# An attention-and-MLP kernel: one item's denominators by another road, one eviction issued earlier, one projection a piece later

## The chip, the cores and the metric

The kernel runs on one core of a Trainium2 chip. A core has a matrix engine (TensorE, "PE" in the profile, with its weight loads as "PEld"), VectorE ("DVE"), ScalarE ("ACT"), GpSimd ("POOL") and SyncE ("SP"), which here only issues DMAs. Each engine works through its own queue in order, and they tell each other of finished work by semaphores. Matrix products write to PSUM, which has eight banks of 512 fp32 numbers per partition; everything else lives in SBUF or in DRAM. The metric is the device time of one execution in microseconds, as the median of the runs.

## The reference, cut to what matters

The input `x` has 16 elements of 256 channels by 32 x 32 positions, so each element is a matrix of 256 channels by S = 1024 positions. All is fp32. Two layers follow one another:

- Layer 0 is an attention with 4 heads of 64 channels: q, k and v by one matrix with a bias, softmax of q times k over the keys, times v, an output matrix `w_out`, and the input added.
- Layer 1 starts with a group norm over 32 groups, then an attention with 8 heads of 32 channels, an output matrix, and its input added; then a second group norm and an MLP of 256 to 1024 to 256 channels with an exact GELU, and its input added.

```python
attn = jax.nn.softmax(jnp.einsum('bihd,bjhd->bijh', q, k) * SCALE, axis=2)
res = jnp.einsum('bijh,bjhd->bihd', attn, v).reshape(B, S, N_HEADS * D_K)
res = res @ w_out + b_out + xs
```

The softmax is computed as exponentials, their sums (the denominators), and a multiplication of the result by the denominators' reciprocals. The kernel takes no maximum off; it keeps running totals of the denominators and of their reciprocals, and runs a general version afterwards if one of them has left the safe range.

## The kernel before, in words

`first_pass` handles the elements b = 0 to 15 one after another. The stages of one element overlap those of its neighbours, and the order is written out by hand: a stage is a Python generator or a list of small functions ("pieces"), and `run` and `run_pieces` call one piece after another. After each piece, `later.tick()` counts down what was put off with `later.after(n, fn)`: fn runs n pieces later. The program text that results is then given to a planner, which lays the instructions into each engine's queue by its own estimate of when each is ready; what stands earlier in the text goes first among those ready. `tc.keep_in_program_order` and `tc.issue_after` tie an instruction behind others of its engine. The waits between engines follow from the tiles that the instructions write and read. The queues in the trace are therefore not exactly the order of the text.

**The first attention** (`attention_a`) has four items per element: two blocks t of 512 positions times two channel halves c. Items are numbered i = 0 to 3 as (t, c) = (0,0), (0,1), (1,0), (1,1). Each item runs over 8 blocks of keys. For each, `scores` forms s_a (line 434) and its exponential e_a (line 444, ScalarE), and two steps later `weigh` accumulates acc_a (line 457, TensorE) and sums the exponentials into es_a (line 471, VectorE). After the last block the result is copied and added from PSUM (lines 477 and 478).

**Its denominators** go one of two roads. The usual one, `denominators` (lines 375 to 406), copies den from PSUM (line 376), spreads four rows of it over 128 partitions by a DMA (line 381), takes the reciprocal of the small 128 x 16 tile (line 387), writes it to DRAM as rows (line 398) and reads these rows back, broadcast to partitions (line 403); two small additions on GpSimd keep the totals (lines 399 and 400). Its `waits` are two numbers of pieces: from the spread to the reciprocal, and from there to the multiplication. `normalise` takes this road for both items of a block t at once, and `scale` multiplies (line 541). The other road, `normalise_item` (lines 489 to 508), is for element 0's block t = 1 alone. It treats each item by itself: den's products (line 493), the reciprocal of the whole 128 x 512 tile on VectorE (line 504), the multiplication (line 505), and `add_to_range` three pieces later, two reductions on VectorE (line 417) and two additions on GpSimd (line 418). For item 2 den is first copied to SBUF (line 502).

**The projections** are made by `out_proj`: o after the first attention, j after the second. Its function `issue` multiplies by the output matrix (`part`, instructions at line 357 through `product`) and evicts with `leave`. A projection of one block t has two column blocks co, each the sum of two products kc. There are two forms. With `apart`, each co has a bank of its own tile, and the order is co by co, each evicted directly. Otherwise both co lie in the two banks of one tile, a "wide" tile; there are three wide tiles, used in turn, and the scores s_b of the second attention use them too. `leave` is on ScalarE (line 781, into a spare tile) where a spare tile is there, which is the case for j of block 0 in elements 1 to 14, and else on VectorE (line 787), with the statistics of the group norm behind it (line 790).

**Between the two attentions** of an element stand, for elements 1 to 14, the previous element's first MLP stage (`hidden`, 12 pieces: begin, middle and finish for each of four parts in pairs; rows "m" of line 1146) and the making of q and k with seven products instead of eight (`qk_by_seven`, line 1052). The second projection of the first attention, o for t = 1, is put off into these pieces by `later.after` in `scale` (line 543). Its statistics start the group norm that makes the second attention's input gn_g.

**The second attention** (`attention_b`) forms s_b (line 602), e_b (line 615), sums es_b (line 630) and acc_b (line 656). Between its units, filler pieces run: the second MLP stage of the previous element, and v of the next one.

Of the kernel before, what the change touches and what calls it, by code (L numbers as in the profile page):

```python
# [259 lines left out]
def first_pass(ctx, tc, x, out, k):  # L260
    nc = tc.nc
    B, C, S = x.shape
    CC, SB, NT = C // P, S // P, S // TB
    HC = k["m1b"].shape[1]
    later = Later()
# [44 lines left out]
    def wide(name, n=None):  # L310
        if n is None:
            n = next(m for m in order if m not in kept)
        use(n)
        return ps_s.tile([P, 2, TB], F32, tag=f"s{n}", name=name)

    def bank(name, n):
        return ps_a.tile([P, TB], F32, tag=f"b{n}", name=name)
# [36 lines left out]
    def product(o, w, r, **flags):  # L354
        for c0 in range(0, P, cols[0]):
            sl = slice(c0, c0 + cols[0])
            nc.tensor.matmul(o[sl], w[:, sl], r, **flags)  # L357
# [17 lines left out]
    def denominators(key, den, d, full, waits, then, parts=1):  # L375
        nc.scalar.copy(d, den)
        n = full.shape[1]
        w = 4 * TB // P
        spread = work.tile([P, w], F32, tag="spread", name=f"sp_{key}", bufs=2)
        row = dram.tile([4 * TB // n, n], F32, tag="row", name=f"row_{key}", bufs=4)  # L380
        nc.sync.dma_start(
            spread, d[:: 32 // parts].rearrange("p (a b) -> p a b", b=w)
        )

        def invert():
            inverse = work.tile([P, w], F32, tag="inverse", name=f"inv_{key}", bufs=2)
            tc.keep_in_program_order(nc.vector.reciprocal(inverse, spread))
            if parts > 1:
                num = P // parts
                for r in range(parts):  # L390
                    nc.sync.dma_start(
                        row[:, r * n // parts : (r + 1) * n // parts].rearrange(
                            "g (a b) -> g a b", b=w
                        ),
                        inverse[r * num : (r + 1) * num],
                    )
            else:
                nc.sync.dma_start(row.rearrange("r (a b) -> (r a) b", b=w), inverse)
            nc.gpsimd.tensor_add(dsum, dsum, spread)
            nc.gpsimd.tensor_add(isum, isum, inverse)  # L400
            num = P * n // (4 * TB)
            for r in range(P // num):
                spread_out["last"] = nc.sync.dma_start(
                    full[r * num : (r + 1) * num], row[r].partition_broadcast(num)
                )
            later.after(waits[1], lambda: then(full))

        later.after(waits[0], invert)
# [5 lines left out]
    def add_to_range(den, inverse):  # L414
        for tot, what in ((dsum, den), (isum, inverse)):
            part = small.tile([P, 1], F32, tag="part", name="part")
            nc.vector.tensor_reduce(part, what, AX.X, ALU.add)
            nc.gpsimd.tensor_add(tot[:, :1], tot[:, :1], part)

    def attention_a(b, qT, kT, v, project):  # L420
        key, D, lag = f"a_{b}", D0, 2
        items = [(t, c) for t in range(NT) for c in range(CC)]
        units = [(i, kb) for i in range(len(items)) for kb in range(SB)]
        res = act.tile([P, CC, S], F32, tag="res", name=f"res_{key}")
# [64 lines left out]
        def normalise_item(i):  # L489
            t, c = items[i]  # L490
            den = wide(f"den_{key}_{i}", next(m for m in order if m != 2))[:, 0, :]
            for j in range(4):
                nc.tensor.matmul(
                    den[j * 32 : (j + 1) * 32, :], k["ones"], sums[i][:, j // 2, :],
                    start=True, stop=True,
                )
            if not c:
                homes.append(act.tile([P, CC, S], F32, tag="k1", name=f"d_{key}_{t}"))
            full, held_den = homes[0][:, c, :TB], homes[0][:, c, TB:]
            r = res[:, c, t * TB : (t + 1) * TB]  # L500
            if c < CC - 1:
                nc.scalar.copy(held_den, den)
                den = held_den
            tc.keep_in_program_order(nc.vector.reciprocal(full, den))
            tc.keep_in_program_order(nc.vector.tensor_mul(r, r, full))
            if c == CC - 1:
                later.after(2, lambda: project(t, res)())
            later.after(3, lambda: add_to_range(den, full))

        def normalise(t):  # L510
            half = TB // 2
# [23 lines left out]
        def scale(t, full):  # L535
            r = res[:, :, t * TB : (t + 1) * TB]
            halves = [
                y.rearrange(form, c=CC, h=2)
                for y, form in ((r, "p c (h q) -> p c h q"), (full, "p (h c q) -> p c h q"))
            ]  # L540
            tc.keep_in_program_order(nc.vector.tensor_mul(halves[0], *halves))
            if t == NT - 1:
                later.after(3 if b else 4, lambda: project(t, res)())

        cols[0] = 32
        pending = []
# [220 lines left out]
    def out_proj(key, w, src, bias, xs, t, stats, then):  # L767
        todo = list(range(CC))

        def issue(cos=range(CC), apart=False):  # L770
            home = None if apart else spare.pop("home", None)
            apart = apart or cols[0] == P
            if not apart:
                both = wide(f"{key}_{t}")
            ps = {}

            def leave(co):
                y = xs[:, co, t * TB : (t + 1) * TB]
                if home is not None:
                    held = home[:, 2 + co]  # L780
                    nc.scalar.activation(
                        held, ps[co], AF.Identity, bias=bias[:, co : co + 1]
                    )
                    later.after(1, lambda: add_up(co, y, held))
                    return
                else:
                    nc.vector.scalar_tensor_tensor(
                        y, ps[co], bias[:, co : co + 1], y, ALU.add, ALU.add
                    )
                nc.vector.bn_stats(stats[:, co, t, :], y)  # L790
                todo.remove(co)

            def add_up(co, y, held):
                with tc.issue_after(spread_out["es"].ins):
                    nc.vector.tensor_add(y, y, held)
                    nc.vector.bn_stats(stats[:, co, t, :], y)

            def part(co, kc):
                product(
                    ps[co],  # L800
                    w[:, kc, co * P : (co + 1) * P],
                    src(kc),
                    start=(kc == 0),
                    stop=(kc == CC - 1),
                )

            for co in cos:
                ps[co] = bank(f"{key}_{t}_{co}", co) if apart else both[:, co, :]
            if apart:
                for co in cos:  # L810
                    for kc in range(CC):
                        part(co, kc)
                    leave(co)
            else:
                for kc in range(CC):
                    for co in cos:
                        part(co, kc)
                for co in cos:
                    leave(co)
            if not todo and then:  # L820
                then()

        return issue
# [208 lines left out]
    def input_sums(key, y):  # L1032
        sums = weights_tile(f"qk7t_{key}")
        b11, b12 = (y[:, 0, t * TB : (t + 1) * TB] for t in range(NT))
        b21, b22 = (y[:, 1, t * TB : (t + 1) * TB] for t in range(NT))
        t1, t2, t3, t4 = (sums[:, n] for n in range(4))
        nc.vector.tensor_sub(t3, b22, b12)
        nc.vector.tensor_sub(t1, b12, b11)
        nc.vector.tensor_sub(t2, b22, t1)
        nc.vector.tensor_sub(t4, b21, t2)  # L1040
        return dict(t1=t1, t2=t2, t3=t3, t4=t4, b11=b11, b21=b21, b22=b22)
# [340 lines left out]
    for b in range(B):  # L1382
        def load_next(b=b):
# [3 lines left out]
            with tc.issue_after(spread_out["last"].ins):  # L1387
                load_blocks(1, b - 1)
                if b + 1 < B:
# [9 lines left out]
                lambda st, b=b, xn=xn, seven=seven, sums_1=sums_1: group_norm(  # L1399
                    f"g{b}", xs[b], st, k["g1w"], k["g1b"], "res", xn, 2 if b else 1,  # L1400
                    (lambda y: sums_1.update(input_sums(f"b{b}", y))) if seven else None,
                ),
# [62 lines left out]
        if first:  # L1465
# [10 lines left out]
                lambda st, b=b, hn=hn: group_norm(  # L1476
                    f"h{b}", xs[b], st, k["g2w"], k["g2b"], "q1", hn,
                    *((3 if b + 1 < B else 1), lambda y, b=b: sums_of_input(b, y)),
                ),
# [305 lines left out]
```

## Time and profile before

| | us |
|---|---|
| median of 3 runs | 3604.61 (3604.31 to 3605.24) |
| the profiled execution | 3603.56 |
| its span, first to last instruction | 3601.8 |
| TensorE busy | 3584.2 |
| VectorE busy | 2786.2 |
| ScalarE busy | 2283.0 |
| GpSimd busy | 219.1 |
| granted TensorE clock | 1.000 |

A row of the timeline gives start and length in us, the engine, the line of the kernel, the operation, output<-inputs by the program's names, and how many instructions were merged. In brackets stands how long the engine was idle before it, and what ended that. Names end in _a for the first attention and _b for the second; o and j are the projections, m the MLP. A product of fp32 numbers shows as two instructions, one for each pass. The ends of products are modelled, since products are pipelined: two rows of one engine may overlap by some 0.1 us, so starts are the better measure. From element 2 on, each element comes 222.4 to 223.8 us behind the one before it.

### The profile page before, as it was taken

The page shows a single profiled execution, that of the slowest core. Times are in us where ns is not written, and L with a number is a line of the kernel's source. Part 1 is how long each engine was busy: PE and PEld are TensorE (multiplying, and loading weights), DVE is VectorE, ACT ScalarE, POOL GpSimd, SP SyncE. Part 2 cuts the span into 40 slices and gives each one's busy share as a digit, 9 for nine tenths or more (in the row PEclk, how much of TensorE's full clock was granted, in tenths as well). Part 3 has the DMA queues.
Part 4 walks back from the last instruction along what each step waited for, and adds up shares of the span by engine and source line. Part 5 has one row for each costly group of instructions (what it writes and reads, how often), then busy time and mean ns, then how long its engine had stood idle before and what let it go on. Part 6 is the DMA issues. An engine that isn't in the chain of part 4 may idle for free.

```text
span 3601.8 us, 81991 instructions
## 1 busy us (share of the span) xinstructions
PE 3584.2 (100%) x35705; PEld 1470.2 (41%) x35705; DVE 2786.2 (77%) x3187; ACT 2283.0 (63%) x3196; POOL 219.1 (6%) x319
## 2 busy tenths in 40 slices
PE   9999999999999999999999999999999999999999
PEld 3334344343444434444344443434434444343433
DVE  5786877868788687876868878688786977868777
ACT  4665757667475675856658566585665757657572
POOL 4000100001000010000000000000000000000000
PEclk9999999999999999999999999999999999999999
DMA  3011311213122131221312213121121212213100
GB/s 130 8 57 33 78 54 38 74 38 83 45 43 69 39 81 45 50 64 36 81 45 52 66 33 81 45 55 63 39 76 45 55 63 47 74 39 64 51 28 28
DMA packets 81137, 197.78 MB, mean 55 GB/s; under 512 B 37666, under 2 KB 38434, under 8 KB 74626
## 3 DMA queue, kind: packets, MB, share of 16 engines
q1 hardware_dynamic: 71392, 163.85, 14.9%
q0 software_dynamic: 7632, 28.21, 5.1%
q8 instruction: 282, 4.62, 0.5%
q14 instruction: 85, 0.70, 0.1%
q10 hardware_dynamic: 1746, 0.40, 0.1%
HBM read 125.32 MB, written 22.27 MB: 41 GB/s over the span
## 4 chain that ended last, share of the span: by engine, by line
PE 92%; DVE 4%; issue 2%; DMA 1%; SPq 1%; ACT 1%; DVEq 0%; POOL 0%
PE s_b L602 12%; PE s_a L434 12%; PE acc_a L457 12%; PE acc_b L656 11%; PE m L357 10%; PE m L1146 10%; PE qk_b L1052 4%; PE qk_a L1052 3%; PE v_b L357 3%; PE j L357 3%; PE v_a L357 3%; PE o L357 3%; PE qk7y_b L1052 1%; PE qk7y_a L1052 1%; DVE es_b L630 1%
## 5 line engine op out<-in xcount | busy, mean ns | idle before, releaser
L615 ACT ACTIVATE e_b<-s_b 128x1024 f32<-128x1024 f32 (+1 forms) x1280 | 981.8, 865 | 135.6 <-PE s_b L602 135.6
L630 DVE TENSOR_TENSOR es_b<-es_b,e_b 128x2048 f32<-128x2048 f32 (+1 forms) x460 | 881.5, 1934 | 104.7 <-ACT e_b L615 88.3
L444 ACT ACTIVATE e_a<-s_a 128x1024 f32<-128x1024 f32 x512 | 520.7, 1024 | 360.3 <-PE s_a L434 359.6
L434 PE MATMUL s_a<-q,k 64*64 64x512 f32 x4096 | 544.5, 593 | 0.7 <-DVE res_a L478 0.7
L457 PE MATMUL acc_a<-e_a,v 64*64 64x512 f32 x4096 | 540.3, 589 | 0.0
L602 PE MATMUL s_b<-q,k 32*64 32x512 f32 x8192 | 527.1, 600 | 2.7 <-ACT v L928 1.3
L471 DVE TENSOR_TENSOR es_a<-es_a,e_a 128x1024 f32<-128x1024 f32 x384 | 469.8, 1224 | 66.0 <-ACT e_a L444 46.5
L656 PE MATMUL acc_b<-e_b,v 128*32 128x512 f32 x4096 | 492.2, 598 | 0.0
L357 PE MATMUL m<-g,w 128*32 128x256 f32 (+2 forms) x6464 | 416.6, 385 | 0.0
L357 PEld LDWEIGHTS m<-g,w 128*32 128x32 f32 (+1 forms) x6464 | 224.7, 111 | 212.0 <-issue 61.8
L457 PEld LDWEIGHTS acc_a<-e_a,v 64*64 64x64 f32 x4096 | 188.2, 133 | 251.2 <-issue 214.9
L602 PEld LDWEIGHTS s_b<-q,k 32*64 32x64 f32 x8192 | 175.9, 130 | 251.0 <-issue 133.0
L434 PEld LDWEIGHTS s_a<-q,k 64*64 64x64 f32 x4096 | 176.0, 133 | 247.5 <-issue 208.1
L656 PEld LDWEIGHTS acc_b<-e_b,v 128*32 128x32 f32 x4096 | 108.5, 109 | 351.5 <-ACT e_b L615 194.7
L630 DVE TENSOR_TENSOR es_b<-e_b,e_b 128x2048 f32<-128x2048 f32 (+1 forms) x72 | 147.0, 2051 | 131.2 <-ACT e_b L615 131.2
L1146 PE MATMUL m<-gn_h,w 128*128 128x512 f32 x512 | 242.5, 602 | 2.7 <-DVE x L1267 1.3
L1210 DVE TENSOR_TENSOR g<-g,g 128x512 f32<-128x512 f32 (+1 forms) x185 | 195.5, 1067 | 1.2 <-PE m L357 0.8
L1146 PE MATMUL m<-hs,w 128*128 128x512 f32 x384 | 178.2, 593 | 0.1
L1161 ACT ACTIVATE g<-g,m1b 128x512 f32<-128x512 f32 x128 | 91.8, 720 | 112.4 <-DVE g L1190 84.5
L1146 PEld LDWEIGHTS m<-gn_h,w 128*128 128x128 f32 x512 | 93.1, 190 | 118.7 <-issue 100.0
L1161 ACT ACTIVATE g<-m,m1b 128x512 f32<-128x512 f32 x128 | 80.9, 683 | 79.0 <-PE m L1146 79.0
L357 PE MATMUL v_a<-wp,x 128*32 128x256 f32 (+1 forms) x1952 | 121.7, 379 | 0.0
(225 smaller groups left out, 3527.9 us busy)
## 6 DMA issues: line engine op xcount, KB each, us to landing
w<-w_kept SPq DMA_DIRECT2D x30, 1792.0 KB
packed_b<-es_b SPq DMA_DIRECT2D x42, 512.0 KB
packed_b<-es_b POOLq DMA_DIRECT2D x42, 512.0 KB, 6.2
rd_b<-row_b SPq DMA_DIRECT2D x252, 64.0 KB
out_dram<-x SPq DMA_DIRECT2D x63, 256.0 KB
d_a<-row_a SPq DMA_DIRECT2D x62, 256.0 KB
x<-in_x_dram SPq DMA_DIRECT2D x30, 512.0 KB
qk<-qk_kept SPq DMA_DIRECT2D x14, 1024.0 KB
```

What stands on the lines that cost most here:

```text
L357: nc.tensor.matmul(o[sl], w[:, sl], r, **flags)
L434: nc.tensor.matmul(s[h : h + HALF, g, :], kT[g * D : (g + 1) * D, c, kb * P + h : kb * P + h + HALF], qT[g * D : (g + 1) * D, c, t * TB : ...
L444: nc.scalar.activation(e, s, AF.Exp, scale=float(D) ** -0.5)
L457: nc.tensor.matmul(accs[i][h][g * D : (g + 1) * D, :], v[h * HALF : (h + 1) * HALF, kb, c * 2 + g], e[h * HALF : (h + 1) * HALF, g, :], st ...
L471: spread_out["es"] = nc.vector.tensor_add(sums[i], held[i] if kb == 1 else sums[i], e)
L602: nc.tensor.matmul(outs[g][h : h + HALF, :], kT[g * D : (g + 1) * D, c, k0 : k0 + HALF], qT[g * D : (g + 1) * D, c, t * TB : (t + 1) * TB] ...
L615: spread_out["exp"] = nc.scalar.activation(to, s, AF.Exp, scale=float(D) ** -0.5)
L630: ins = nc.vector.tensor_add(d, (d if kb else es[0][:, g : g + step]), es[m][:, g : g + step])
L656: nc.tensor.matmul(acc[g * D : (g + 1) * D, :], v[:, kb + m, c * G + g], es[m][:, g, :], start=(m == 0), stop=(m == 1),)
L1052: nc.tensor.matmul(to, w, x[right], start=first, stop=True, skip_group_check=not first)
L1146: nc.tensor.matmul(ps, blocks[1][number - 1][:, i * P : (i + 1) * P], inputs[b][number], start=first, stop=True, skip_group_check=not first,)
L1210: (nc.vector.tensor_add if plus else nc.vector.tensor_sub)(d, d, more)
```

## The change

There are three edits.

1. In `normalise_item`, item 2 of element 0 no longer takes the reciprocal of its whole tile on VectorE. It calls `denominators` with waits (2, 2) and multiplies when the broadcast rows are back. For item 3 the road stays; the two reductions are tied behind its multiplication.
2. In `out_proj`, for projections in a wide tile, the eviction of a column block is issued directly after that block's own last product. Before, both evictions were issued after all products. The order of the products is the same.
3. In `scale`, the second projection o is put off by 4 pieces instead of 3 in elements 1 to 15. Element 0 does not come through this line for t = 1, since `normalise_item` serves it.

```diff
             r = res[:, c, t * TB : (t + 1) * TB]
+
+            def scale_item(full):
+                return tc.keep_in_program_order(nc.vector.tensor_mul(r, r, full))
+
             if c < CC - 1:
-                nc.scalar.copy(held_den, den)
-                den = held_den
+                denominators(f"{key}_{i}", den, held_den, full, (2, 2), scale_item)
+                return
             tc.keep_in_program_order(nc.vector.reciprocal(full, den))
-            tc.keep_in_program_order(nc.vector.tensor_mul(r, r, full))
-            if c == CC - 1:
-                later.after(2, lambda: project(t, res)())
-            later.after(3, lambda: add_to_range(den, full))
+            scaled = scale_item(full)
+            later.after(2, lambda: project(t, res)())
+
+            def to_range():
+                with tc.issue_after(scaled.ins):
+                    add_to_range(den, full)
+
+            later.after(3, to_range)
...
             if t == NT - 1:
-                later.after(3 if b else 4, lambda: project(t, res)())
+                later.after(4, lambda: project(t, res)())
...
                 for kc in range(CC):
                     for co in cos:
                         part(co, kc)
-                for co in cos:
-                    leave(co)
+                        if kc == CC - 1:
+                            leave(co)
```

## The prediction

> **What bounds the kernel now.** I read the page first, then the chain of waits on TensorE, then the timeline engine by engine around each of the three edits. The page says where time can be:
>
> ```profile
> PE 3584.2 (100%) x35705; PEld 1470.2 (41%) x35705; DVE 2786.2 (77%) x3187; ACT 2283.0 (63%) x3196; POOL 219.1 (6%) x319
> ```
>
> TensorE is busy for 3584.2 of 3601.8 us. Only 17.6 us are visibly idle: 12.7 in gaps, 4.8 after its last product. The view of TensorE's waits names the gaps; these three lie near the edits (columns: total us, times, longest).
>
> ```profile
> PE den_a L493 <- DVE es_a L471: 2.6, 1, 2.6
> PE o L357 <- DVE res_a L541: 1.5, 2, 0.8
> ...
> PE m L1146 <- DVE g L1174: 0.7, 4, 0.2
> ```
>
> If the busy row were exact, the change could win 4.8 us here at most. But a busy row can hide a stall, so I compared how long the same group of products takes in different places. TensorE's timeline in element 1's second attention (start, us, engine, line):
>
> ```profile
> 414.90 1.98 PE L602 MATMUL s_b<-q,k 32*64 32x512 f32 x32
> 416.80 1.92 PE L656 MATMUL acc_b<-e_b,v 128*32 128x512 f32 x16
> 418.54 3.67 PE L357 MATMUL j<-res_b,wpj 128*32 128x512 f32 x32
> 422.15 2.54 PE L602 MATMUL s_b<-q,k 32*64 32x512 f32 x32
> ```
>
> Both s_b rows are the same 32 score products. From their start to the next row it is 1.90 us at 414.90 and 2.47 us (422.15 to 424.62) behind the projection j. All 14 middle elements have it: 2.47 behind j each time, against 1.90 to 1.91 in 143 other places. That is 0.566 us x 14 = 7.9 us which no list of gaps shows. The rows of j's eviction (line 781) and ScalarE's timeline give the cause:
>
> ```profile
> 422.29 1.26 ACT L781 ACTIVATE packed_b<-j,pjb 128x512 f32<-128x512 f32 x2 [1.96 <-PE j L357]
> ```
> ```profile
> its engine sat idle before it (us, times) until:
>   PE j L357: 28.1, 14
> who waited for it (us, times):
>   PEld s_b L602: 5.5, 14
> ```
>
> ScalarE idles 2 us until all 32 products of j are done, then evicts both banks in a row. The scores want that pair of banks and wait.
>
> **What the Trainium skill says.** "Perfetto Trace Analysis", Identifying the Most-Contended Engine, says matmul busy time is no good measure of distance from the limit; the hidden 0.57 us agrees. "TensorE: Matmul & The Clock Gate", Step-by-step, says only weight loads are pulled ahead and matmuls stay in program order, so products behind the waiting scores cannot pass; here acc_b begins late, at 424.62. "PSUM — Partial Sum Buffer", The four PSUM rules, calls each bank a separate SRAM, so evicting one bank while products fill the other is allowed; the trace does it at 534.05, where q<-qk_a is evicted from one bank while a product begun at 533.42 fills the other bank of that tile. "DMA: Bandwidth & Descriptors", Latency and other measured facts, puts a DMA's fixed cost at about 2 us; den's spread in element 0 took 2.05 (copy ended 61.02, its first reader ran at 63.07).
>
> **Part 2, the eviction behind its own product (lines 818 and 819).** Nothing is added or removed: two evictions, the same 32 products. Column block 0's last products start at 420.75 and end at 421.36, block 1's start at 421.61 and end at 422.22. Now the first eviction starts at 422.286, 0.067 behind the end of block 1, and the second ends at 423.551. With the eviction issued behind its own block, the first runs at 421.43 to 422.12 and the second at 422.29 to 422.97, so the banks are free 0.58 us sooner. ScalarE has nothing else then (idle from 420.33), so the earlier start displaces no work. TensorE now runs the second half of the scores two by two: four products at 423.06, four at 423.49, then the waiting four at 423.60 and at 424.08. Elsewhere these are eight and eight. Upper end: with the banks free at 422.97 the eight go together at 423.06, and all 0.566 returns. Lower end: the split order stays, and only the wait from 423.51 to 423.60 goes, 0.09. In the value I take, the eight go together but their weights load late: a start behind a late wait comes 0.534 us after the one before instead of 0.429, so 0.105 is lost and 0.46 won. Fourteen times: 6.5 us, ends 1.3 and 7.9. I take the grouped form because a single eviction behind the last product is what filler pieces have already: at 410.32 and 415.81 the eight go together. The projections of elements 0 and 15 are followed by acc_b, which takes its 1.74 us and does not want those banks: 0.
>
> **Part 1, the third item of element 0.** VectorE's timeline, then TensorE's:
>
> ```profile
> 77.57 3.35 DVE L504 RECIPROCAL d_a<-d_a 128x512 f32<-128x512 f32 x1
> 80.83 1.16 DVE L471 TENSOR_TENSOR es_a<-es_a,e_a 128x1024 f32<-128x1024 f32 x1
> 81.91 0.68 DVE L505 TENSOR_TENSOR res_a<-res_a,d_a 128x512 f32<-128x512 f32 x1
> 82.51 1.27 DVE L417 TENSOR_REDUCE part<-d_a 128x1 f32<-128x512 f32 x2
> 83.69 5.20 DVE L471 TENSOR_TENSOR es_a<-es_a,e_a 128x1024 f32<-128x1024 f32 x4
> ```
> ```profile
> 83.72 2.75 PE L457 MATMUL acc_a<-e_a,v 64*64 64x512 f32 x24
> 89.05 1.06 PE L493 MATMUL den_a<-es_a,ones 128*32 128x512 f32 x8 [2.58 <-DVE es_a L471]
> ```
>
> The 128x512 reciprocal and two reductions, 3.35 + 1.27 = 4.62 us, push four sums behind their inputs, and den_a waits 2.58 us for the last. The change takes these out and puts in a 128x16 reciprocal (0.25, row of line 387), two additions on idle GpSimd (0.21 and 0.22), and six issues on SP, whose queue is empty between 67.3 and 110: spread (0.70), row (0.33), four broadcasts (1.8 for four at 3511.96). The multiply (0.68) stays. From 77.66 VectorE then has five sums, 0.25 and 0.68, or 7.0 us, and the last input is ready at 84.98: the last sum can end at 86.25, before TensorE's 86.47. Full win: 2.58. Against it stands the multiply's position. Spread back at 79.25, inverse 79.5, broadcasts issued from about 81.1 (row issue plus the 1.45 seen at 64.68 to 66.13). Broadcasts of this size reached a waiting multiply 3.85 to 7.59 us after their first issue in element 1 and later; element 0 has little traffic then, so about 85. If the multiply stands before the last sum, that ends at 86.9, den_a follows 0.16 later as it does now, and 0.6 is given back; before the last two, 1.8; before three, the wait grows by 0.4; at 7.59, by some 4. I take 1.9, ends 2.6 and -4. The last item's chain is next: its reciprocal (3.36) starts when den_a ends or when line 478 ends, at worst 0.3 us later relative to TensorE, where 0.2 is slack. Its reductions are only tied behind the multiply, and cost nothing.
>
> **Part 3, the second projection one piece later (elements 1 to 15).** TensorE's timeline in element 1, and the idle time before line 541:
>
> ```profile
> 282.27 4.45 PE L1146 MATMUL m<-hs,w 128*128 128x512 f32 x10
> 287.57 3.70 PE L357 MATMUL o<-res_a,wo 128*128 128x512 f32 x8 [0.85 <-DVE res_a L541]
> ```
> ```profile
> its engine sat idle before it (us, times) until:
>   DMA d_a<-row_a: 25.3, 15
> ```
>
> In program text o stands before the piece finish(1). But the ten m<-hs products are finish(0), finish(1) and one product of the next piece: o was already issued behind finish(1), because its data come late. Moving it behind that piece in the text should leave TensorE's queue as it is; it moves no DMA, and no SP or GpSimd issue. Its eight products, four evictions and statistics, and the norm chain all come a piece (1.7 us) later at most; that chain's gn_g is ready at 525.4 in element 2, and qk_b takes it at 534.4. Only two elements stalled (0.85 and 0.64), both with late row transfers (3.6 and 3.3 us from row issue to broadcast, 1.5 usually). Ends: +1.5 and, if VectorE's order suffers, -2: it is packed from 508.2 to 517.8 and has 0.6 us before a product waits for line 1174. I take 0.3.
>
> **Sum.** 6.5 + 1.9 + 0.3 = 8.7 us. The profiled execution took 3603.56 (span 3601.8 and 1.76 around it), giving 3594.9; the median is 1.05 above it: 3595.9.
>
> **The rivals.** (a) The split order stays: 1.3 + 1.9 = 3.2 us, 3601.4. For it: the queue's order is fixed ahead by planned durations that I cannot see. Against: the filler pieces above. (b) The multiply blocks VectorE in element 0: with part 2 whole, 6.5 + 0.3 - 0.4 = 6.4, 3598.2. For it: line 541 waited for its DMA with VectorE idle 15 times. (c) Slower: the first eviction makes block 1's last products wait, if a tile is guarded as a whole. They would start at 422.27 (eviction's end 422.12, 0.05 for the signal, 0.1 for weights) instead of 421.18: 1.09 us x 16 = 17.4, less 6.5 and 1.9: 9.0 slower, 3613.6. It decides above 0.98 us each. For it: now the first eviction waits for the whole tile. Against: the qk case at 533.42. (d) The change does nothing where it matters, because evictions were held by ScalarE: excluded by its 2 us of idleness.
>
> **How the numbers follow.** A measurement of this kernel can tell 0.2%, 7.2 us, from no change: below 3597.4 is faster, above 3611.8 slower. Main case 0.60, own range 3592 to 3599 (parts 5.5 to 7.9, 0.4 to 2.6, 0 to 1.5), nine tenths of it faster. (a) 0.14 and (b) 0.11, mostly within, (b) at its best faster. (c) and other added stalls 0.15, nearly all slower. So faster is 0.54 + 0.04 = 0.58, same 0.06 + 0.14 + 0.07 + 0.01 = 0.28, slower 0.14. The range 3590.5 to 3604 takes in the main case with its bounds, (a) and (b), and leaves out (c).
>
> **What would show it.** Right: line 781 starts 0.9 us before j's last product ends, s_b behind j takes 1.90 to 2.05, and den_a L493 loses most of its 2.6. Wrong: s_b stays at 2.3 or more (a), j itself grows to 4.5 (c), or VectorE idles for d_a around 82 to 86 (b). If o runs in another place among the m products, part 3 is not neutral. The forecast fails if the planned order changes elsewhere by 0.5 us per element.

## The result, and the profile after

The kernel after takes 3618.81 us (median of 6 runs, 3617.27 to 3619.64), the kernel before 3604.90 in the same session (3603.47 to 3605.33): 13.9 us longer, a ratio of 1.0039 with a 95% interval of 1.0026 to 1.0052. The forecast was 3595.9, with a range to 3604.0; the change is slower, by more than the 0.2% that can be told. Rival (c) had the sign, but neither its size nor all of its cause.

The page of the kernel after, TensorE's row. The span is 3617.8 us, 16.0 more than before; the busy time rose by 12.7, with the same 35705 instructions.

```profile
PE 3596.9 (99%) x35705; PEld 1468.4 (41%) x35705; DVE 2785.1 (77%) x3185; ACT 2285.7 (63%) x3196; POOL 219.0 (6%) x319
```

Most of the loss is again no visible gap: it stands as "busy". The waits of TensorE (total us, times, longest) show what is visible: a new wait of qk_a in 14 elements, den_a's wait nearly as long as before, more waits of j, and o's wait shorter.

```profile
PE qk_a L1060 <- DVE g L1199: 2.7, 14, 0.2
PE den_a L493 <- DVE es_a L471: 2.4, 1, 2.4
PE j L357 <- DVE res_b L745: 2.2, 6, 0.5
...
PE o L357 <- DVE res_a L549: 0.5, 1, 0.5
```

The waits of j for its scaled result (line 745) were 0.4 us before. In the thirteen executions profiled for this document, one for each kernel, they lie between 0.3 and 2.2 us and follow no single edit, so they are not counted as an effect of one.

**Around the eviction (part 2).** TensorE's timeline in element 1, where 32 products of j once stood in one block and 32 score products behind them (line 789 is now what line 781 was, line 610 what 602 was; products are counted by their instructions, as in the prediction):

```profile
420.39 2.92 PE L357 MATMUL j<-res_b,wpj 128*32 128x512 f32 x24
423.24 1.07 PE L610 MATMUL s_b<-q,k 32*64 32x512 f32 x2
424.24 1.07 PE L357 MATMUL j<-res_b,wpj 128*32 128x512 f32 x8
425.23 1.97 PE L610 MATMUL s_b<-q,k 32*64 32x512 f32 x30
```

ScalarE's timeline of the same place, and, from the view of line 789, who waited for it:

```profile
423.38 0.69 ACT L789 ACTIVATE packed_b<-j,pjb 128x512 f32<-128x512 f32 x1 [1.20 <-PE j L357]
```
```profile
who waited for it (us, times):
  PEld j L357: 11.4, 14
  PEld s_b L610: 3.5, 14
```

The first eviction does stand behind its own product. But j's last eight products, which fill the other bank of the tile, now wait for it: the eviction ends at 424.06 and they start at 424.24. Two score products stand ahead of them in TensorE's queue; the other thirty come last. The second eviction starts at 425.37, when j's eight are done. From the start of j to acc_b (427.13 here): by starts, 2.69 us where j itself isn't held up (as in element 3), then 1.00, 1.00 and 1.90, or 6.58, where the kernel before took 3.55 + 2.47 = 6.02. That is 0.56 us in each of 14 elements, 7.8 us.

**Around the second projection (part 3).** VectorE's timeline in element 2, before and after; line 787, now 795, is the first eviction of o. Before, it stood ahead of the second addition of finish(1) (line 1191, now 1199) and two of the combining subtractions (line 1210, now 1218); now it stands behind that addition and one of them:

```profile
512.58 0.74 DVE L787 SCALAR_TENSOR_TENSOR x<-o,bvo,x 128x512 f32<-128x512 f32 x1
513.25 0.68 DVE L1191 TENSOR_TENSOR g<-g,m 128x512 f32<-128x512 f32 x1
```
```profile
515.09 0.68 DVE L1199 TENSOR_TENSOR g<-g,m 128x512 f32<-128x512 f32 x1
515.69 0.69 DVE L1218 TENSOR_TENSOR g<-g,g 128x512 f32<-128x512 f32 x1
516.29 0.75 DVE L795 SCALAR_TENSOR_TENSOR x<-o,bvo,x 128x512 f32<-128x512 f32 x1
```

On TensorE, 15 us later, a qk_a product starts late, again before and after:

```profile
528.19 1.02 PE L1052 MATMUL qk7y_a<-qk7t_a,wp 128*128 128x512 f32 x2
529.05 1.11 PE L1052 MATMUL qk_a<-x,wp 128*128 128x512 f32 x2
```
```profile
530.69 1.02 PE L1060 MATMUL qk7y_a<-qk7t_a,wp 128*128 128x512 f32 x2
531.91 1.12 PE L1060 MATMUL qk_a<-x,wp 128*128 128x512 f32 x2 [0.20 <-DVE g L1199]
```

From the start of one to that of the other it is 1.22 us instead of 0.86. What leads there is a chain on VectorE: the evictions come later, so do the group norm's means, gn_g and the input sums qk7t_b, and the additions of the next part (lines 1198 and 1199) queue behind these; qk_a's bank is free only when line 1199 has read it (it ends at 531.86, qk_a starts at 531.91). In TensorE's queue gm_g stands one m product (two instructions) later than before, so the rearrangement is in both queues.

**Around the third item (part 1).** VectorE, then TensorE, in element 0:

```profile
86.01 0.69 DVE L503 TENSOR_TENSOR res_a<-res_a,d_a 128x512 f32<-128x512 f32 x1 [2.73 <-DMA d_a<-row_a]
```
```profile
89.31 1.06 PE L493 MATMUL den_a<-es_a,ones 128*32 128x512 f32 x8 [2.38 <-DVE es_a L471]
90.17 5.34 PE L357 MATMUL o<-res_a,wo 128*32 128x512 f32 x32
```

The 4.6 us of reciprocal and reductions are gone, but the multiplication (line 503) waits 2.73 us for its broadcast rows, with two sums (86.62 to 89.17) behind it. The four broadcasts began to issue at 81.58, and the last landed about 4.4 us later. The gap before den_a is 2.38 instead of 2.58.

### The profile page after: what moved, and what is told of

Same layout as the page of the kernel before. It is cut to its first block, busy times and chain, and to the rows that moved or that the text cites. A ratio compares the mean times of both kernels' runs of the same rounds, so it can differ in the third digit from the quotient of the medians.

```text
span 3617.8 us, 82016 instructions
## 1 busy us (share of the span) xinstructions
PE 3596.9 (99%) x35705; PEld 1468.4 (41%) x35705; DVE 2785.1 (77%) x3185; ACT 2285.7 (63%) x3196; POOL 219.0 (6%) x319
## 4 chain that ended last, share of the span: by engine, by line
PE 78%; issue 10%; DVE 7%; DMA 2%; SPq 1%; ACT 1%; POOL 0%; DVEq 0%; POOLq 0%; ACTq 0%
PE s_a L434 12%; PE acc_a L457 12%; PE s_b L610 11%; PE acc_b L664 10%; PE m L357 9%; PE qk_b L1060 3%; PE qk_a L1060 3%; PE v_b L357 3%; PE j L357 3%; PE v_a L357 2%; DVE es_b L638 2%; PE m L1154 2%; PE o L357 2%; PE qk7y_b L1060 1%; DMA rd_b<-row_b 1%
## 5 line engine op out<-in xcount | busy, mean ns | idle before, releaser
L1181 ACT ACTIVATE g<-m 128x512 f32<-128x512 f32 x64 | 38.2, 597 | 133.3 <-PE m L1154 133.3
```

## The experiments

The theory formed from these traces: part 2 costs about 10 us because the wide tile is guarded as a whole, part 3 about 4 because VectorE's order changed, and part 1 nothing. Each kernel is compared with the kernel before on the same chip. Where two lines of measured values are close, the intervals (about 0.1% to either side) say how close they can be told.

### One part at a time

```diff
 # p1_only: the first hunk of the change alone
 # p2_only: the hunk in out_proj alone
 # p3_only
-                later.after(3 if b else 4, lambda: project(t, res)())
+                later.after(4, lambda: project(t, res)())
```

> The third item's new road alone, the two other edits left out. Theory (the loss of 14 us lies in the eviction and in the second projection; the new road is neutral, because its multiplication stands before the last two sums and waits for its DMA): -0.5 to +0.3 us against before; den_a's wait for the sums stays at 2.2 to 2.6 us, and line 503 waits 2 to 3 us for d_a. Rival (this edit carries part of the loss, by o's first products at half rate behind that wait): +1 to +2.5 us, with o in element 0 starting its products 0.85 us apart instead of 0.43.

> The eviction behind its own product alone. Theory (the wide tile is guarded as a whole, so column block 1's last products wait for block 0's eviction): +9 to +11 us (0.72 us in each of 14 elements), j's last eight products in elements 1 to 14 wait for ScalarE's line 781, two score products run before them. Rival (the loss came from the projection a piece later, and the eviction gives what I forecast): -6.5 us.

> The second projection one piece later alone. Theory (o keeps its place on TensorE, but its evictions go behind the MLP's additions on VectorE, the norm chain is late and qk_a waits): +3.5 to +5.5 us (0.38 us in each of 14 elements, less 1 to 2 us of stalls that go). Rival (neutral, as forecast): -2 to +1.5 us, and the rest of the 14 us is in the other edits or in their sum.

| part alone | median us | before | difference | ratio, 95% interval |
|---|---|---|---|---|
| 1, third item | 3603.43 | 3603.47 | -0.04 | 0.9992 to 1.0009 |
| 2, eviction | 3613.59 | 3603.47 | +10.12 | 1.0016 to 1.0037 |
| 3, second projection | 3607.22 | 3603.47 | +3.75 | 1.0001 to 1.0018 |

The sum is 13.83, the whole change 13.9: the parts add, and the three theories held as to the times. Part 2's trace has the same pattern of 24, 2, 8 and 30 products, but 0.56 us longer in each of 14 elements, not the 0.72 expected: 7.8 us. The rest is in elements 0 and 15, which evict on VectorE and lose as well. TensorE's timeline of element 15 with part 2 alone:

```profile
3531.59 2.76 PE L357 MATMUL j<-res_b,wpj 128*32 128x512 f32 x24
...
3537.76 1.06 PE L357 MATMUL j<-res_b,wpj 128*32 128x512 f32 x8 [0.75 <-DVE x L787]
...
3539.61 2.84 PE L357 MATMUL m<-g,w 128*128 128x512 f32 x6
```

From j's start to the m products it is 8.02 us, where the kernel before takes 6.49 for the same 56 instructions: 1.53 more. In element 0 the like stretch takes 7.17 instead of 6.12. Together 7.8 + 1.5 + 1.1 = 10.4, against 10.1 measured; waits that vary from one execution to the next, such as j's for its scaled result, are left out of this sum.

For part 3 the traces give this account: qk_a's interval grew from 1.72 to 2.08 us and the next one from 1.80 to 1.82, 5.3 us in 14 elements; o's own wait for line 541 fell from 1.5 to 0.5, and m's wait for line 1174 (0.7) went. 5.3 - 1.0 - 0.7 = 3.6, and 3.75 was measured. The 5.3 belong to the edit. The other two may not: o's wait is 0.5 to 0.6 in `p1_only` and `p2_only` too, which leave this edit out, and the interval (0.4 to 6.5 us) takes in both sums.

### The guard taken away: two tiles

Each column block gets a wide tile of its own, whose second bank stays unused. Products, evictions and biases are the same. In `two_tiles` the eviction comes behind its own product, as in the change; in `two_tiles_late` both are issued behind all products in the program text, as before.

```diff
-            if not apart:
-                both = wide(f"{key}_{t}")
...
-                ps[co] = bank(f"{key}_{t}_{co}", co) if apart else both[:, co, :]
+                ps[co] = bank(f"{key}_{t}_{co}", co) if apart else wide(f"{key}_{t}_{co}")[:, 0, :]
```

> The second edit with each column block of the wide projection in a wide tile of its own (its second bank unused), so that no guard of a whole tile stands between the first eviction and the other block's products. The two other edits are left out. Theory (the 10 us came from the guard of the whole tile, and the earlier eviction is worth what I forecast once that is gone): j's last eight products start 0.43 us behind the ones before, without a wait for line 779; the score products behind j take 1.90 to 2.05 us to the next row instead of 2.47; -4 to -7 us against before. Rival (the hardware cannot fill one bank while the eviction of another runs, or the early eviction itself disturbs the order): j still takes 4 us or more and the time is +5 us or more above before.

> The same two wide tiles for the projection, but with both evictions behind all products as in the kernel before. Theory (the scores behind j waited for both banks of one tile; with two tiles only the first eviction, which ends at the same time as the first scores' second half needs its bank, stands before them): between -4 and -7 us, within 1.5 us of the kernel with two tiles and the early eviction, so the early eviction is then worth nothing of its own. Rival (the early eviction is what frees the banks): 0 us, scores behind j at 2.4 to 2.5 us as before.

`two_tiles` took 3596.61 us against 3603.46, 6.85 less (ratio 0.9973 to 0.9987); `two_tiles_late` 3596.07, 7.39 less (0.9972 to 0.9987), somewhat more than the 4 to 7 expected. With two tiles and the eviction behind its own product, TensorE's timeline and ScalarE's in element 1:

```profile
419.84 3.74 PE L357 MATMUL j<-res_b,wpj 128*32 128x512 f32 x32
423.51 1.97 PE L602 MATMUL s_b<-q,k 32*64 32x512 f32 x32
```
```profile
422.79 0.69 ACT L779 ACTIVATE packed_b<-j,pjb 128x512 f32<-128x512 f32 x1 [1.17 <-PE j L357]
```

The first eviction starts at 422.79, 0.8 us before the last of j's products ends. No product waits for it, and the scores behind j take 1.90 us in all 14 elements. So one bank can be evicted while products fill another (the Trainium skill, "PSUM — Partial Sum Buffer", The four PSUM rules, calls the banks separate SRAMs, and this run agrees): it is the tile that was guarded. The same place with both evictions behind all products in the text, TensorE and ScalarE of `two_tiles_late`:

```profile
417.81 3.68 PE L357 MATMUL j<-res_b,wpj 128*32 128x512 f32 x32
```
```profile
420.70 0.69 ACT L779 ACTIVATE packed_b<-j,pjb 128x512 f32<-128x512 f32 x1 [1.10 <-PE j L357]
```

The eviction is not late here: in both kernels, in all 14 elements, the first one starts 0.79 us before the last of j's products ends. With a tile of its own, a block is evicted when its own products are done, wherever the text has the eviction. So the place in the text is worth nothing with two tiles. But the expectation of `two_tiles_late` took it for a kernel with late evictions, and it is none: what the earlier eviction is worth by itself was not tested. Counted from j's start, where nothing holds j up, the second eviction ends after 4.37 us in both, instead of 4.95 in the kernel before. These 0.58 us are the gain in time that the prediction had counted on; the shared tile had kept it from coming. The scores' weight loads still wait for that eviction, but it ends 0.08 us before the second half of the scores starts, and no product is late.

### VectorE's order restored: the combining subtractions put off

The third edit, and with it the two combining subtractions of finish(1) issued one piece later, behind o in the text. `put_off` puts the subtractions off and leaves o at the earlier piece.

```diff
-            combine((1, 0), (0, 0), False, i)
-            combine((0, 1), (1, 1), False, i)
+            def combines():
+                combine((1, 0), (0, 0), False, i)
+                combine((0, 1), (1, 1), False, i)
+
+            if i == 1:
+                later.after(1, combines)
+            else:
+                combines()
```

> The third edit alone, and with it the two combining additions of the MLP's second part (line 1210) put off by one piece, so that they stand behind the second projection in the program text. Theory (the 3.75 us are VectorE's: the projection's evictions and statistics queue behind these additions, the norm chain is late and qk_a waits): the first eviction comes 1 us earlier in its element again, qk_a's wait for line 1191 goes, and the time is -1 to +1 us against before. Rival (the piece itself is late for the projection, whatever VectorE does): +3 to +5 us, as with the third edit alone.

> Only the two combining additions of the MLP's second part put off by one piece; the second projection stays a piece earlier as in the kernel before. Theory (what matters is that they do not stand ahead of the projection's evictions on VectorE, and in the kernel before they cost nothing): -1 to +1 us against before. Rival (they delay the norm chain in the kernel before too): -2 us or less.

`p3_put_off` took 3603.04 us against 3603.46 (0.9990 to 1.0007), `put_off` 3603.65 against 3603.98 (0.9991 to 1.0007): both no different from before. The loss of part 3 is gone although o stands at the later piece, so the piece itself is not what cost. VectorE's timeline in element 2 with the subtractions put off:

```profile
514.50 0.75 DVE L787 SCALAR_TENSOR_TENSOR x<-o,bvo,x 128x512 f32<-128x512 f32 x1
515.52 0.75 DVE L787 SCALAR_TENSOR_TENSOR x<-o,bvo,x 128x512 f32<-128x512 f32 x1 [0.28 <-PE o L357]
...
517.49 0.64 DVE L1216 TENSOR_TENSOR g<-g,g 128x512 f32<-128x512 f32 x1
```

With the third edit alone the first eviction has a subtraction (line 1210, here 1216) right ahead of it, and another between it and its statistics. Here two subtractions come behind both statistics. The first eviction itself came only 0.6 us earlier, not 1: counted from the start of line 541 it follows after 4.40 us in the kernel before, 5.82 with the third edit alone and 5.26 here. But the second statistics, which the norm waits for, end after 8.26, 9.88 and 8.23 us: all of the delay is gone. The wait of qk_a for line 1191, 2.8 us in 14 elements with the third edit alone, does not occur any more, and its interval is 1.72 us again.

TensorE's queue is not the same in these runs either, since the planner orders both engines, and the traces show what part it has. Counted from o's start in element 2, in the kernel before, with the third edit alone and here: VectorE has the means ready after 7.21, 8.61 and 7.00 us, and TensorE's product gm_g, which takes them up, starts after 8.58, 9.44 and 7.72. With the third edit alone the means just miss gm_g's old place, and it stands one m product (0.86 us) later. So VectorE's order begins the delay, and TensorE's order hands it on: gv_g, the next product of the norm, starts after 10.52, 11.38 and 10.52, line 1191 after 17.72, 18.09 and 17.72. It was not tried to change VectorE's order with TensorE's fixed.

### The multiplication put off

```diff
 # in the first hunk of the change; p1_late has (2, 4), p1_later5 has (2, 5)
-                denominators(f"{key}_{i}", den, held_den, full, (2, 2), scale_item)
+                denominators(f"{key}_{i}", den, held_den, full, (2, 5), scale_item)
```

> The third item's new road alone, with the multiplication put off by four pieces instead of two, so that one of the last two sums stands before it on VectorE. Theory (the gap before den_a is set by the multiplication that waits for its DMA ahead of two sums): line 503 waits less, den_a's wait falls from 2.4 to 0.6 to 1.2 us, and the time is 1.2 to 1.8 us below before. Rival (the sums' inputs or TensorE's order set the gap): den_a's wait stays above 2 us and the time is unchanged.

> The first edit alone with the multiplication put off by five pieces: it stands behind all sums on VectorE, behind the last item's own reciprocal. Theory (a multiplication waiting for its DMA ahead of the sums is all that was left of den_a's gap; its row has arrived long before it is needed): den_a's wait for the sums falls to under 0.3 us, -2 to -3 us against before, a further 0.5 to 1.5 below the one put off by four pieces unless the last item's multiplication, now one place later, makes o wait. Rival (that multiplication makes the second half of o late by 0.7 us or more): no better than put off by four.

`p1_late` took 3601.02 us against 3603.47 (0.9985 to 1.0002), `p1_later5` 3600.86 against 3603.46 (0.9984 to 1.0001): 2.5 and 2.6 less, with intervals that just take in no change. With four pieces the gap shrank less than expected and the time more: den_a still waited 1.54 us, not 0.6 to 1.2, since one sum stood behind a multiplication that waited 1.45; a part of the difference may be the clock's (last section). With five the gap was none at all. TensorE's timeline with five, where nothing stands in brackets behind den_a:

```profile
86.24 1.07 PE L493 MATMUL den_a<-es_a,ones 128*32 128x512 f32 x8
```

So the gap was the multiplication's place, as the theory said. In the medians, removing all of the gap was no better than removing a part (0.2 us, where 0.5 to 1.5 was expected). The traces show where a part of it went. With five pieces the last item's multiplication comes later too, and the second half of o stands behind eight instructions of qk_a instead of four. These keep TensorE busy, but the norm behind o is late, and TensorE waits for it:

```profile
103.94 7.13 PE L357 MATMUL qk_b<-gn_g,wq 128*128 128x512 f32 x16 [0.40 <-DVE gn_g L893]
```

With four pieces qk_b does not wait. den_a starts 1.61 us earlier with five than with four (86.24 against 87.85), but v_b behind qk_b only 0.94 earlier (110.91 against 111.85). So the rival was right in kind, with qk_b in the place of o. What goes after that, in o's and j's waits of later elements, varies from one execution to the next, and the intervals, some 3 us to either side, do not settle it.

### Joined

`best1` is five pieces for the third item and two tiles, with both evictions behind all products in the text; `best2` has the third edit and the put-off subtractions besides.

```diff
 # best1: the first hunk of the change, with
+                denominators(f"{key}_{i}", den, held_den, full, (2, 5), scale_item)
 # and in out_proj
+                ps[co] = bank(f"{key}_{t}_{co}", co) if apart else wide(f"{key}_{t}_{co}")[:, 0, :]
 # best2: besides, in scale and in finish
+                later.after(4, lambda: project(t, res)())
+                later.after(1, combines)
```

> Two parts joined that touch different places: the third item's new road with its multiplication put off by five pieces, and the middle projections in two wide tiles with both evictions behind all products; the second projection stays where it was. Theory (the gains add, since den_a's gap lies in element 0 and the scores behind j in elements 1 to 14): -2.6 and -7.4, so -9 to -11 us against before. Rival (the same later wait bounds both): -7 us or less.

> The same as the joined kernel, and with it the second projection one piece later with the combining additions put off behind it (worth -0.4 us alone, within its interval of nothing). Theory (that pair is neutral once VectorE's order is restored): within 1 us of the joined kernel, -9 to -11.5 us against before. Rival (with the earlier rhythm of the second attention, the later projection costs again): 3 us or more above the joined kernel.

`best1` took 3594.49 us against 3603.98, 9.5 less (0.9961 to 0.9984); `best2` 3592.32, 11.7 less (0.9956 to 0.9980). The gains add. `best2` is below `best1` by 2.2 us, more than the 1 us expected. Its trace has shorter waits of o (0.6 against 1.1) and of j (0.9 against 1.9), and lacks a wait of qk_a for k's eviction (1.0); but these are waits of single executions, which vary, so the difference is not explained. `best2` is faster than the kernels before and after, and its page has TensorE busy for 3575.6 us, 8.6 less than before, with the same 35705 instructions.

## Why the prediction was wrong

**The sum.** -6.5, -1.9 and -0.3 were forecast; +10.1, 0.0 and +3.75 were measured.

**Part 2: the step that failed is "the trace does it at 534.05".** The sentence took two operations for one tile's two banks because the profile names both qk_a. Names leave buffer numbers out, and the code of `qk_by_seven` takes one wide tile per channel half (`both = wide(f"qk7_{key}_{ch}")`). By the order of the pieces in the code and the wait shown below, the eviction at 534.05 belongs to one half, the product at 533.42 to the other. The case that did bear on it stood next to it in the trace of the kernel before, ScalarE's timeline and TensorE's:

```profile
534.57 0.69 ACT L1060 ACTIVATE k<-qk_a,bqk 128x512 f32<-128x512 f32 x1 [1.22 <-PE qk_a L1052]
```
```profile
533.42 1.11 PE L1052 MATMUL qk_a<-x,wp 128*128 128x512 f32 x2
...
535.31 1.12 PE L1052 MATMUL qk_a<-qk7t_a,qk 128*128 128x512 f32 x2
```

Line 1060 evicts the bank that the product at 533.42 filled, and ends at 535.25. The product at 535.31 fills the other bank of that same tile (in `qk_by_seven` the piece p5 of a half comes behind its p2). It starts 0.05 us behind the eviction's end, 0.94 after the qk_b product between them (534.37) instead of 0.86. A guard of the whole tile was there to be seen. The 534.05 case was the sole evidence against rival (c), for which the wait of the first eviction for all products already spoke.

Rival (c) had the mechanism, and its size was off: 1.09 us each in 16 elements, less 6.5 and 1.9 gained elsewhere. The products did start about a microsecond late, but two score products slipped in between, and the scores behind took 1.90 us instead of 2.47: the second eviction, at 426.06 in element 1, ends just before their second half starts (426.14). So 0.56 each in 14 elements. In elements 0 and 15, which the prediction set at 0 because acc_b "does not want those banks", the one that waits is j itself: 1.05 and 1.53 us, behind VectorE's eviction. The prediction's hidden 0.57 us behind j was real (its 143 places with 1.90 to 1.91 us are those behind products of m; in all there are 220, and 14 behind den_b take 2.35, which no edit touched), and 7.4 of its 7.9 us can be had, but by giving j two tiles instead of moving the eviction in the text.

**Part 3: the place of o was right, the value was not.** "Moving it behind that piece in the text should leave TensorE's queue as it is" held for o: the same ten m<-hs products stand before it. What failed is the step from there to 0.3 us. The prediction followed only o's data and had gn_g ready 9 us ahead of qk_b (525.4 against 534.4), but named the wrong reader. The chain reaches TensorE through VectorE's queue: the additions of the next part stand behind gn_g's input sums, and qk_a needs the bank that they read. Its bad end, -2, was "if VectorE's order suffers"; that case came, with 5.3 us of new waits, against which at most 1.7 of stalls went.

**Part 1: the ends were right, the choice was not.** The prediction named that the multiplication "before the last two" would give back 1.8 of 2.58. It stood there. The broadcasts issued when they should: at 81.58 in an execution that ran 0.46 us later here (den_a could have started at 86.93, before at 86.47), against 81.1 foretold. But their journey took 4.4 us where 3.9 was assumed. So 1.8 + 0.5 = 2.3 was given back, and the gap is 2.38. Two terms were mis-sized, the place (1.8 given back) and the journey (0.5). The sign that the prediction named for rival (b) came as well: VectorE idled for d_a, from 83.28 to 86.01. The choice of 1.9 over rival (b) assumed that the planner would put the multiplication behind all sums but the last, and no row spoke for that.

**The chances.** Case (c) had 0.15 together with other added stalls, because the 534.05 case seemed to exclude it. Without that case the evidence was a wait for the whole tile on the evicting side, and (c) should have stood above the main case.

## What to carry to other kernels

In this kernel an eviction could run ahead of other products only when these were in another tile: the guard followed the tile as it was allocated, not the bank, and a wait appeared that nobody wrote. With a tile for each block, the eviction's place in the text no longer mattered. Before a row of the trace is used as proof that two operations overlap in one buffer, look up in the code which buffer each has, since names hide it. And before a kernel is taken as the late case of a comparison, look up in its trace whether the step is late. When a step is moved without changing its place on the busy engine, look at the order of the engine that consumes it, and follow that queue to the next thing that the busy engine wants from it, not only along the step's own data.

## What the runs showed of the hardware beyond that

The first products of o in element 0 took 5.27 us in the profile after, against 3.57 before. They were not waiting: the granted clock fell. The windows view of the kernel after (length, then busy us of TensorE, weight loads, VectorE, ScalarE, GpSimd, each with its instructions, then the granted clock, and DMA):

```profile
90.00:91.00 1.00, 1.00 (x12) 0.43 (x8) 0.56 (x1) 0.00 (x0) 0.00 (x0) 0.78 0.00 0
91.00:92.00 1.00, 1.00 (x8) 0.27 (x4) 1.00 (x1) 0.00 (x0) 0.00 (x0) 0.50 0.00 0
```

It runs at half from 90.57 to 93.98, for 3.41 us, and then at full speed again. Of the nine profiled executions in which den_a's gap was 2.4 to 2.6 us, four show it (o at 5.0 to 5.3 us) and five do not, the kernel before among the five; the four have kernels with and without each of the edits among them; of the four in which it was 1.5 us or none, none does.

The traces can tell why only some do. The granted clock rises some microseconds into each execution: at 5.23 us here, where the starts of the first products (named warm) go from 0.85 to 0.43 us apart. In the four executions that show it, the clock drops 85.33 to 85.34 us after that rise, and stays low for 3.41 us, which is a twenty-fifth of that. So I lay a grid of 3.41 us from the rise over all thirteen executions, and ask how much of den_a's gap lies in one step of it. It is 2.16, 2.25, 2.58 and 2.58 us in these four, and in the nine others at most 1.99 (1.31 to 1.99 in the six that have a gap, the kernel before with 1.86, nothing in the three without one). A gap of one length thus costs nothing or 1.7 us, by where it lies on the grid. This is read from the traces afterwards; no run set the gap's place. The Trainium skill, "TensorE: Matmul & The Clock Gate", What's actually happening, gives an idle window of some 3.4 us, free-running, as what throttles the array. The step agrees with that, but it did not have to be idle as a whole: 2.16 us of it were enough here, and 1.99 were not.

The times show it too. Of the 105 executions of the kernel before that the experiments were compared with, 38 have a mean granted clock of 0.999 instead of 1.000, and in the median they took 1.4 to 1.5 us longer than the others. Of the 39 executions of the four kernels with a gap of 1.5 us or none, not one has it. (The mean is rounded, and an execution with the drop can stand at 1.000, as the profiled one of `p2_only` does.) So closing the gap also saves this, which an account by gaps leaves out. It is one reason, with j's waits, why the profiled spans differ by 16.0 us and the medians by 13.9.
